# Two attention blocks on one core: exponential sums kept in the first block's own place, the last projection's products in turn, and the last norm's scalings queued behind other readers

## Chip, cores, metric

One core of a Trainium2 chip runs the whole program. The metric is the device time of one execution in microseconds (us). In what follows PE is TensorE (matmuls), DVE is VectorE, ACT is ScalarE, POOL is GpSimd, SP is the queue that issues most DMAs, PSUM is the memory that PE accumulates in (eight banks of 128 x 512 float32) and SBUF the on-chip memory that the other engines work in.

## The reference

The input is 8 images of 32 x 32 tokens with 512 channels, float32. Two layers run one after the other, each adding to its input:

```python
x = x + L0(gn(x))   # qkv = xt @ w_qkv; 16 heads of 32 channels; softmax(q k^T / sqrt(32)) v; @ w_proj + b
x = x + L1(gn(x))   # q, k, v by Wq, Wk, Wv; 4 heads of 128; scores + relative position logits; softmax; @ Wo
```

`gn` is a group norm over 32 groups of 16 channels. Softmax is over the 1024 keys.

## The kernel before

**Layout.** Activations are held transposed, channels on partitions: four chunks of 128 channels by 1024 tokens. Each 512 x 512 projection is done by a seven-product scheme (a two by two split of both operands with seven instead of eight half-size products). The sums of activations that it needs are made by `forming` (L343 to L371) as four DVE operations of 128 x 1024: s1, s2, a fresh a21 and s4. A product (`taken`, L385) reads one of these seven operands; product 5 needs s2, product 6 the fresh a21, product 2 needs s4, product 3 only a raw quarter. Results gather in three PSUM tiles x, y and z. Between two products of one tile another engine must have read it: `p1` (an ACT copy of x after product 0), `a` (a DVE add from y after product 5), `b` (the same after product 4), `p7` (an ACT copy of z after product 6). Class `Onto` (L536) adds the results to the running activations, and `put_out` (L1031) transposes 128 x 512 pieces on DVE and stores each with four DMAs, in the last image half of them from ACT's queue.

**Layer 0 attention** (`attention_0`, L632 to L702) walks, for each image, over 8 groups (4 chunks of heads by 2 halves of queries) and in each over 8 key blocks. For a block, `front` makes the scores of four heads by 8 matmuls into one PSUM tile `ps` of four banks, of which there is a single one, and ACT turns it into exponentials `e` (128 x 2048) at L653. A step later, `back` multiplies `e` with the values into `acc` (L664) and DVE adds `e` to the group's sum (L679). The tiles `e` have two buffers under the tag e0, and the sum `es` has one buffer of its own under es0. The first sum of a group, at its second block, reads the first two `e` and writes `es`. The later ones add one `e` to `es`. At the end `finish` sums `es` over partitions by a matmul (L689) and `normalise` (L602) makes the reciprocals and scales the result, its last operation being a POOL multiply (L630).

**Layer 1 attention** (`attention_1`, L754) does the same for four heads of 128, with smaller tiles; its last group also ends in `normalise`.

**Order.** PE always has other work to put beside an attention: `side_by_side` weaves the steps of layer 0 attention of image b with the projections of the images before and after. Within that, the framework's scheduler orders each engine's instructions when the program is made, by priority of tracing and by its own idea of when operands are ready. Two handles override it: `tc.issue_after(ins)` puts what is traced in it behind `ins` on that engine (order alone, no wait), and `tc.keep_in_program_order(ins)` puts one instruction behind everything traced before it on its engine. `by_columns` (L327) uses the latter while `in_place[0]` is set, for the four instructions of its next call.

**The end.** After the last attention nothing is left to weave. `after_last` (L1058) runs the last image's output projection by `in_two_parts` (L485): products 0 and 1 of both column halves u, which read query half 0, and then for each u `five_last` (L459) with products 5, 4, 6, 2, 3. The image before it goes through `after_1` (L1020) with the last image's second norm (`norm_1`, L978, `group_norm`, L265) woven in; the norm's four scalings (L304) are queued behind the newest layer 0 sum.

Of the kernel before, what the change touches and what calls it, by code (L numbers as in the profile page):

```python
# [27 lines left out]
def quick_path(  # L28
# [140 lines left out]


    ORDER = [0, 5, 1, 4, 6, 2, 3]
    FIRST_TWO, LAST_FIVE = [0, 1], [5, 4, 6, 2, 3]

    class Stream:

# [167 lines left out]
    def forming(x, name, room=None, behind=None, into=None):  # L343


        a11, a12 = x[:, :HC, :NB], x[:, HC:, :NB]
        a21, a22 = x[:, :HC, NB:], x[:, HC:, NB:]
        if room is not None:
            s1, s2, s4 = [room[:, i, :].rearrange("p (c n) -> p c n", n=NB) for i in range(3)]
        else:  # L350
            s1, s2, s4 = [
                mem.tile([P, HC, NB], F32, tag=f"form{i}", name=f"f{i}_{name}", bufs=1)
                for i in (1, 2, 4)
            ]
        fs = [a11, a12, s4, a22, s1, s2, a21]
        if into is not None:
            into.extend(fs)
        for i, (op, out, one, other) in enumerate((
            (nc.vector.tensor_add, s1, a21, a22),
            (nc.vector.tensor_sub, s2, s1, a11),  # L360
            (nc.vector.tensor_sub, a21, a11, a21),
            (nc.vector.tensor_sub, s4, a12, s2),
        )):

            late = None
            if behind is not None:
                late = behind[i]() if isinstance(behind, tuple) else behind()
            with tc.issue_after(late.ins) if late is not None else nullcontext():
                last_form[0] = op(out, one, other)
            yield 0  # L370
        return fs  # L371
# [110 lines left out]
        sink.c22(b, p7)  # L482
        yield HC

    def in_two_parts(x, m, sinks, name, room=None, done=lambda u: None, behind=None):  # L485

        early = [x[:, :HC, :NB], x[:, HC:, :NB]]
        p1s, fs = [], []
        sums = forming(x, name, room, behind, fs)

        def products():
            for u in range(2):
                stream.unit(m, False, u)
                p1s.append((yield from two_first(early, u, sinks[u], f"{name}_{u}")))

        def beside(u):
            if u == 0:
                yield from sums
                return

            with tc.issue_after(begun[0].ins):
                done(0)
            yield 0

        yield from woven(products(), (next(sums) for _ in range(2)), 0, 1)
        for u in range(2):
            stream.unit(m, False, u)
            yield from woven(five_last(fs, u, sinks[u], f"{name}_{u}", p1s[u]), beside(u), 0, 1)
        done(1)

    class Plain:
# [87 lines left out]
                hook if u else None,  # L599
            )  # L600

    def normalise(dst, acc_sums, name):  # L602

        su = mem.tile([P, NB], F32, tag="rec", name=f"su_{name}", bufs=2)
        nc.scalar.copy(su, acc_sums)  # L608
        turned = mem.tile([P, NB], F32, tag="rec", name=f"tu_{name}", bufs=2)
        nc.vector.transpose(turned, su)  # L610
        few = turned.rearrange("p (t c) -> p t c", c=32)[:, :, 0]
        rec = mem.tile([P, NB // 32], F32, tag="few", name=f"rc_{name}", bufs=2)
        nc.vector.reciprocal(rec, few)
        at = check_at[0]
        check_at[0] += 1
        nc.vector.tensor_tensor_reduce(
            out=few,
            in0=few,
            in1=rec,
            op0=ALU.add,  # L620
            op1=ALU.max,
            scale=1.0,
            scalar=0.0,
            accum_out=checks[:, at : at + 1],
        )
        nc.vector.transpose(  # L626
            su.rearrange("p (t c) -> p t c", c=32),
            rec.unsqueeze(2).to_broadcast([P, NB // 32, 32]),
        )
        nc.gpsimd.tensor_tensor(dst, dst, su, op=ALU.mult)  # L630

    def attention_0(q, k, v, b, blocks=range(NT)):  # L632

        steps = [(m, h, j) for m in (0, 2, 1, 3) for h in range(NH) for j in blocks]
        state = {}

        def front(m, h, j):
            name = f"0_{b}_{m}_{h}_{j}"
            ps = psum.tile([P, HB, NB], F32, tag="ps", name=f"ps_{name}", bufs=1)
            for i in range(2):  # L640

                some = slice(64 * i, 64 * i + 64)
                for r in range(HB):
                    rows = slice(r * D0, (r + 1) * D0)
                    nc.tensor.matmul(  # L645
                        ps[some, r, :],
                        k[m][rows, j * P + 64 * i : j * P + 64 * i + 64],
                        q[m][rows, h * NB : (h + 1) * NB],
                        start=True,
                        stop=True,  # L650
                    )
            e = mem.tile([P, HB, NB], F32, tag="e0", name=f"e_{name}", bufs=2)
            nc.scalar.activation(e, ps, AF.Exp, scale=D0 ** -0.5)  # L653
            return e

        def back(m, h, j, e):
            name = f"0_{b}_{m}_{h}_{j}"
            if j == blocks[0]:
                state["acc"] = psum.tile([P, NB], F32, tag="acc", name=f"acc_{name}", bufs=1)
                state["first"] = e  # L660
            acc = state["acc"]
            for r in range(HB):
                c0 = (m * HB + r) * D0
                nc.tensor.matmul(  # L664
                    acc[r * D0 : (r + 1) * D0, :],
                    v[:, j, c0 : c0 + D0],
                    e[:, r, :],
                    start=(j == blocks[0]),
                    stop=(j == blocks[-1]),
                )  # L670
            if j == blocks[1]:
                state["esum"] = mem.tile([P, HB, NB], F32, tag="es0", name=f"es_{name}", bufs=1)
                other = state["first"]
            elif j != blocks[0]:
                other = state["esum"]
            if j != blocks[0]:

                with tc.issue_after(reader[0].ins) if beside_norm[0] else nullcontext():
                    summed[0] = nc.vector.tensor_add(state["esum"], other, e)  # L679
            if j != blocks[-1]:  # L680
                return
            nc.scalar.copy(q[m][:, h * NB : (h + 1) * NB], acc)
            state["ended"] = (m, h, state["esum"])

        def finish(m, h, esum):
            name = f"0_{b}_{m}_{h}"
            su = psum.tile([P, NB], F32, tag="acc", name=f"sums_{name}", bufs=1)
            for r in range(HB):
                nc.tensor.matmul(  # L689
                    su[r * D0 : (r + 1) * D0, :],  # L690
                    ones[:, :D0],
                    esum[:, r, :],
                    start=True,
                    stop=True,
                )
            normalise(q[m][:, h * NB : (h + 1) * NB], su, name)

        pending = None
        for at in steps:
            if "ended" in state:  # L700
                finish(*state.pop("ended"))
            e = front(*at)  # L702
            if pending is not None:
                back(*pending)
            pending = (*at, e)
            yield 2
        back(*pending)
        yield 1
        finish(*state.pop("ended"))
# [44 lines left out]
    def attention_1(q, k, v, posT, b, beside=0):  # L754
# [38 lines left out]
        def finish(h, c, esum):  # L793
# [17 lines left out]
            su = psum.tile([P, HB, NB], F32, tag="ps", name=f"sums_{name}", bufs=1)[:, 0, :]  # L811
            nc.tensor.matmul(su, ones_r, greater, start=True, stop=False)
            nc.tensor.matmul(su, ones_r, rest, start=False, stop=True)
            normalise(q[:, h, c * NB : (c + 1) * NB], su, name)

        pending = None
        ending = []
# [240 lines left out]
    def after_last(b, st):  # L1058

        x = st["ao"]  # L1060
        xT = fetch(st["kept"], block(f"x2T_{b}"))
        sinks = [Onto(halves(xT, u), then=put_out(b, st, xT, u)) for u in range(2)]
        run(in_two_parts(x, WO, sinks, f"wo_{b}"))

    def woven(main, side, start, gap, places=(0,)):

        for at, cost in enumerate(main):
            if at >= start and (at - start) % gap in places:
                cost += next(side, 0)
            yield cost  # L1070
        yield from side
# [46 lines left out]
    def units(m, rows=False):  # L1118
        return [(m, rows, u, ORDER) for u in range(2)]

    def in_parts(m):
        return [(m, False, u, some) for some in (FIRST_TWO, LAST_FIVE) for u in range(2)]

    FIRST = units(WQ0) + units(WK0) + units(WV0, True)
    plan = [(m, m is WV0, u, ORDER) for u in range(2) for m in (WV0, WQ0, WK0)]
    for b in range(B + 1):
# [7 lines left out]
            plan += units(WQ1) + units(WK1) + units(WV1, True)  # L1134
        if b + 1 < B:
            plan += FIRST if b else units(WQ0) + units(WK0)[:1] + units(WV0, True)
    plan += in_parts(WO)

    states = [{} for _ in range(B)]
    load_first(states[0])  # L1140
# [21 lines left out]
    for b in range(B + 1):  # L1162
# [11 lines left out]
        if last is not None:  # L1174
            if past is not None:
                norm = norm_1(
                    b - 1, last, after=lambda: half_done[0], behind=lambda: summed[0]
                )
                if coming is not None:
                    norm = chain(norm, later(sums_1, b - 1, last))  # L1180
# [536 lines left out]
```

## Time and profile before

| what | value |
|---|---|
| median of 3 runs | 3826.51 us (3825.41 to 3826.73) |
| profiled execution, its own time | 3826.55 us |
| its span | 3824.8 us |
| mean granted PE clock | 0.998 |
| PE busy | 3786.5 us, 99% of the span |
| DVE busy | 2564.1 us, 67% |
| ACT busy | 1761.1 us, 46% |
| POOL busy | 658.5 us, 17% |

The span is from the first to the last instruction on the chip; the execution's own time is 1.75 us longer. A group row of the profile gives line, engine, operation, tiles written and read, shapes and count; then busy time and the mean of one; then the idle time of the engine just before these instructions and what ended it. A timeline row gives start and length in us, then the same names, with idle time in square brackets. A row of the table of waits reads "who waited <- for whom: total us, times, longest".

### The profile page before, as it was taken

Reading aid. Unit: us, or ns where it says so; the run is one execution under the profiler, and the core shown is the slowest. Engines: PE = TensorE matmul, PEld = TensorE weight load, DVE = VectorE, ACT = ScalarE, POOL = GpSimd, SP = SyncE. Lnnn points to the kernel's source line nnn. Section 1 sums busy time; section 2 is a strip of 40 time slices with the busy share of each in tenths; the row PEclk is TensorE's granted clock in tenths of the full one; section 3 lists DMA queues with packets and bytes.
Section 4 is the critical chain, followed back from the end, with each engine's and each line's share of the span. In section 5 each row is a group of like instructions: output and inputs, shape, how many; then the busy total and the mean of one; then the engine's idle time right before and its main releaser. Section 6 shows DMA issues by size and latency. Waiting matters only on the chain.

```text
span 3824.8 us, 79906 instructions
## 1 busy us (share of the span) xinstructions
PE 3786.5 (99%) x34478; PEld 1377.5 (36%) x34478; DVE 2564.1 (67%) x2966; ACT 1761.1 (46%) x1830; POOL 658.5 (17%) x398
## 2 busy tenths in 40 slices
PE   9999999999999999999999999999999999999998
PEld 4222244322443234432343323433234332334353
DVE  6778665686756866569665686656866568665544
ACT  2554544445444454444544445444454445553132
POOL 1342101131011310013111131111310112001201
PEclk9999999999999999999999999999999999999999
DMA  6132120242202312023120241103411033110311
GB/s 186 62 110 63 41 56 7 65 108 56 56 12 89 87 49 56 16 92 92 39 53 19 93 96 40 45 23 98 90 42 39 27 98 76 32 37 32 111 38 26
DMA packets 482985, 234.74 MB, mean 61 GB/s; under 512 B 269600, under 2 KB 461376, under 8 KB 481600
## 3 DMA queue, kind: packets, MB, share of 16 engines
q1 hardware_dynamic: 470992, 213.74, 20.5%
q0 software_dynamic: 2608, 13.70, 1.0%
q8 instruction: 274, 4.49, 0.5%
q10 hardware_dynamic: 9024, 2.10, 0.3%
q14 instruction: 87, 0.71, 0.1%
HBM read 170.72 MB, written 58.72 MB: 60 GB/s over the span
## 4 chain that ended last, share of the span: by engine, by line
PE 92%; DVE 4%; ACT 2%; issue 1%; DMA 0%; SPq 0%; POOL 0%; DVEq 0%; ACTq 0%; POOLq 0%
PE ps L645 13%; PE acc L664 12%; PE ps L764 12%; PE acc L776 12%; PE y_q L331 4%; PE y_v L331 4%; PE y_k L331 4%; PE ps L765 3%; PE x_q L331 3%; PE x_v L331 3%; PE z_k L331 3%; PE z_q L331 3%; PE x_k L331 3%; PE z_v L331 3%; ACT e L653 2%; DVE es L679 2%
## 5 line engine op out<-in xcount | busy, mean ns | idle before, releaser
L653 ACT ACTIVATE e<-ps 128x2048 f32<-128x2048 f32 x512 | 961.8, 1879 | 816.3 <-PE ps L645 631.3
L679 DVE TENSOR_TENSOR es<-es,e 128x2048 f32<-128x2048 f32 x384 | 891.1, 2321 | 380.7 <-ACT e L653 378.4
L645 PE MATMUL ps<-q,k 32*64 32x512 f32 x8192 | 577.7, 613 | 11.3 <-ACT e L653 11.3
L664 PE MATMUL acc<-e,v 128*32 128x512 f32 x4096 | 545.8, 604 | 0.0
L767 ACT ACTIVATE e<-ps 128x512 f32<-128x512 f32 x512 | 305.7, 597 | 507.2 <-PE ps L765 437.7
L764 PE MATMUL ps<-q,k 128*128 128x512 f32 x1024 | 525.0, 594 | 0.3 <-DVE posT L750 0.3
L776 PE MATMUL acc<-e,v 128*128 128x512 f32 x1024 | 522.0, 593 | 0.7 <-ACT e L767 0.7
L630 POOL TENSOR_TENSOR q<-q,su 128x512 f32<-128x512 f32 x128 | 201.6, 1575 | 1536.2 <-DVE su L626 1412.1
L787 DVE TENSOR_TENSOR es<-es,e 128x512 f32<-128x512 f32 x384 | 290.5, 757 | 251.3 <-ACT e L767 248.0
L765 PE MATMUL ps<-posT,sel 128*128 128x512 f32 x512 | 406.6, 794 | 0.0
L764 PEld LDWEIGHTS ps<-q,k 128*128 128x128 f32 x1024 | 192.5, 190 | 230.2 <-issue 218.5
L645 PEld LDWEIGHTS ps<-q,k 32*64 32x64 f32 x8192 | 120.4, 129 | 403.4 <-issue 211.8
L776 PEld LDWEIGHTS acc<-e,v 128*128 128x128 f32 x1024 | 193.1, 189 | 147.7 <-issue 92.6
L664 PEld LDWEIGHTS acc<-e,v 128*32 128x32 f32 x4096 | 81.3, 108 | 411.4 <-issue 364.1
L679 DVE TENSOR_TENSOR es<-e,e 128x2048 f32<-128x2048 f32 x64 | 177.3, 2770 | 31.9 <-ACT e L653 31.8
L610 DVE STREAM_TRANSPOSE tu<-su 128x512 f32<-128x512 f32 x128 | 90.6, 708 | 97.7 <-ACT su L608 96.1
L765 PEld LDWEIGHTS ps<-posT,sel 128*128 128x128 f32 x512 | 97.3, 190 | 122.5 <-issue 122.5
L608 ACT COPY su<-sums 128x512 f32<-128x512 f32 x128 | 74.9, 585 | 130.4 <-PE sums L689 80.6
L534 POOL TENSOR_TENSOR k<-b_k,p_k 128x512 f32<-128x512 f32 x32 | 51.2, 1601 | 479.4 <-ACT p_k L434 468.6
L750 DVE TENSOR_TENSOR posT<-pp,posT 32x512 fp32r<-32x512 f32 x128 | 111.9, 875 | 32.2 <-ACT posT L745 30.9
L745 ACT CAST posT<-pp 32x512 fp32r<-32x512 f32 x128 | 106.1, 829 | 46.4 <-PE pp L732 45.3
L534 POOL TENSOR_TENSOR v<-b_v,p_v 128x512 f32<-128x512 f32 x32 | 51.6, 1614 | 433.7 <-ACT p_v L434 433.7
(223 smaller groups left out, 4606.6 us busy)
## 6 DMA issues: line engine op xcount, KB each, us to landing
w_qkv<-ws_qkv SPq DMA_DIRECT2D x168, 128.0 KB, 2.3
d<-x0T SPq DMA_DIRECT2D x32, 512.0 KB, 3.2
x1T<-d SPq DMA_DIRECT2D x32, 512.0 KB, 5.9
d<-x1T SPq DMA_DIRECT2D x32, 512.0 KB, 3.6
x2T<-d SPq DMA_DIRECT2D x32, 512.0 KB, 6.4
w_qkv<-in_L_conv_w_qkv SPq DMA_DIRECT2D x126, 128.0 KB, 2.2
out<-ot SPq DMA_DIRECT2D x240, 64.0 KB, 2.0
xs<-in_x SPq DMA_DIRECT2D x224, 64.0 KB, 2.4
```

The source lines that it names most:

```text
L331: ins = nc.tensor.matmul(out[columns, :], weights[:, columns], moving, start=start, stop=stop, skip_group_check=open_sum,)
L630: nc.gpsimd.tensor_tensor(dst, dst, su, op=ALU.mult)
L645: nc.tensor.matmul(ps[some, r, :], k[m][rows, j * P + 64 * i : j * P + 64 * i + 64], q[m][rows, h * NB : (h + 1) * NB], start=True, stop=True,
L653: nc.scalar.activation(e, ps, AF.Exp, scale=D0 ** -0.5)
L664: nc.tensor.matmul(acc[r * D0 : (r + 1) * D0, :], v[:, j, c0 : c0 + D0], e[:, r, :], start=(j == blocks[0]), stop=(j == blocks[-1]),)
L679: summed[0] = nc.vector.tensor_add(state["esum"], other, e)
L750: nc.vector.tensor_sub(rest, logits, greater)
L764: nc.tensor.matmul(ps, k[h][:, keys], q[:, h, queries], start=True, stop=False)
L765: nc.tensor.matmul(ps, sel_flat[:, keys], posT[:, h, queries], start=False, stop=True)
L767: nc.scalar.activation(e, ps, AF.Exp, scale=1.0 / math.sqrt(D1))
L776: nc.tensor.matmul(acc, v[:, j, h * D1 : (h + 1) * D1], e, start=(j == 0), stop=(j == NT - 1),)
L787: added[0] = nc.vector.tensor_add(state["esum"], state["esum"], e)
```

## The change

Sums of layer 0: the two `e` buffers and the `es` buffer become one tile of three places. The first exponential of a group is written to one place and becomes the group's sum there; the later exponentials take turns in the other two; the next group's first one takes the next place in turn, and the old sum's place joins the turn behind it. The last output projection: products 0 of both halves, then products 1 of both, with three of `forming`'s operations traced beside them instead of two, then a new function `five_alone` with the order 5, 6, 4, 3, 2, each product's first four matmuls kept in program order; `forming`'s fourth operation is queued behind the add `a`. The very last `normalise` multiplies on DVE instead of POOL. In the last round the norm's scalings are queued behind the newest add `a` or `b` (`reader`) instead of the newest layer 0 sum.

```diff
-    FIRST_TWO, LAST_FIVE = [0, 1], [5, 4, 6, 2, 3]
+    FIRST_TWO, LAST_FIVE, LAST_ALONE = [0, 1], [5, 4, 6, 2, 3], [5, 6, 4, 3, 2]
...
-                late = behind[i]() if isinstance(behind, tuple) else behind()
+                late = behind[i] if isinstance(behind, tuple) else behind
+                late = late() if late is not None else None
...
+    def five_alone(fs, u, sink, name, p1):
+        product = taken(fs, u, False)
+        y = bank(f"y_{name}")
+        in_place[0] = True
+        product(y, 5, True)
+        a = snapshot("es1", f"a_{name}")
+        begun[0] = nc.vector.tensor_add(a, y, p1)
+        sink.early(p1, a)
+        yield HC
+        z = bank(f"z_{name}")
+        in_place[0] = True
+        product(z, 6, True)
+        p7 = snapshot("e1", f"p7_{name}")
+        nc.scalar.copy(p7, z)
+        yield HC
+        in_place[0] = True
+        product(y, 4, False)
+        b = snapshot("es1", f"b_{name}")
+        nc.vector.tensor_add(b, y, p1)
+        sink.middle(b)
+        yield HC
+        in_place[0] = True
+        product(z, 3, False)
+        sink.c21(z, a)
+        sink.c22(b, p7)
+        yield HC
+        in_place[0] = True
+        product(y, 2, False)
+        sink.c12(y, p1)
+        yield HC
...
         def products():
+            if in_turn:
+                base = stream.at + 1
+                parts = [two_first(early, u, sinks[u], f"{name}_{u}") for u in range(2)]
+                for i in range(4):
+                    stream.at = base + i % 2
+                    yield next(parts[i % 2])
...
-        yield from woven(products(), (next(sums) for _ in range(2)), 0, 1)
+        begin, rest = (3, five_alone) if in_turn else (2, five_last)
+        yield from woven(products(), (next(sums) for _ in range(begin)), 0, 1)
...
-        nc.gpsimd.tensor_tensor(dst, dst, su, op=ALU.mult)
+        engine.tensor_tensor(dst, dst, su, op=ALU.mult)
+
+    e_room = mem.tile([P, 3, HB, NB], F32, tag="e0", name="e_room", bufs=1)
+    turn, sum_at = [0, 1], [2]
...
-            e = mem.tile([P, HB, NB], F32, tag="e0", name=f"e_{name}", bufs=2)
+            at = turn.pop(0)
+            if j == blocks[0]:
+                turn.append(sum_at[0])
+                sum_at[0] = at
+            else:
+                turn.append(at)
+            e = e_room[:, at]
...
             if j == blocks[1]:
-                state["esum"] = mem.tile([P, HB, NB], F32, tag="es0", name=f"es_{name}", bufs=1)
-                other = state["first"]
-            elif j != blocks[0]:
-                other = state["esum"]
+                state["esum"] = state["first"]
...
-                    summed[0] = nc.vector.tensor_add(state["esum"], other, e)
+                    summed[0] = nc.vector.tensor_add(state["esum"], state["esum"], e)
...
+            end = (b, h, c) == (B - 1, H1 - 1, NH - 1)
+            normalise(
+                q[:, h, c * NB : (c + 1) * NB], su, name, nc.vector if end else nc.gpsimd
+            )
...
-        run(in_two_parts(x, WO, sinks, f"wo_{b}"))
+        run(in_two_parts(x, WO, sinks, f"wo_{b}", behind=(None, None, None, lambda: begun[0]), in_turn=True))
...
-    plan += in_parts(WO)
+    plan += in_parts(WO, LAST_ALONE)
...
-                    b - 1, last, after=lambda: half_done[0], behind=lambda: summed[0]
+                    b - 1,
+                    last,
+                    after=lambda: half_done[0],
+                    behind=lambda: (summed if here is not None else reader)[0],
```

More of the change, by code (lines that the diff above doesn't have):

```diff
@@ L483, in five_last, with in_two_parts @@
         yield HC
-    def in_two_parts(x, m, sinks, name, room=None, done=lambda u: None, behind=None):
+    def five_alone(fs, u, sink, name, p1):
[28 more added lines that the diff above has]
+        yield HC
+    def in_two_parts(
+        x, m, sinks, name, room=None, done=lambda u: None, behind=None, in_turn=False
+    ):
         early = [x[:, :HC, :NB], x[:, HC:, :NB]]
@@ L491, in products @@
         def products():
+            if in_turn:
[4 more added lines that the diff above has]
+                    yield next(parts[i % 2])
+                for part in parts:
+                    try:
+                        next(part)
+                    except StopIteration as end:
+                        p1s.append(end.value)
+                return
             for u in range(2):
@@ L503, in beside @@
             yield 0
-        yield from woven(products(), (next(sums) for _ in range(2)), 0, 1)
+        begin, rest = (3, five_alone) if in_turn else (2, five_last)
+        yield from woven(products(), (next(sums) for _ in range(begin)), 0, 1)
         for u in range(2):
             stream.unit(m, False, u)
-            yield from woven(five_last(fs, u, sinks[u], f"{name}_{u}", p1s[u]), beside(u), 0, 1)
+            yield from woven(rest(fs, u, sinks[u], f"{name}_{u}", p1s[u]), beside(u), 0, 1)
         done(1)
@@ L600, in project_rows, with normalise @@
             )
-    def normalise(dst, acc_sums, name):
+    def normalise(dst, acc_sums, name, engine=nc.gpsimd):
         su = mem.tile([P, NB], F32, tag="rec", name=f"su_{name}", bufs=2)
@@ L813, in finish @@
             nc.tensor.matmul(su, ones_r, rest, start=False, stop=True)
-            normalise(q[:, h, c * NB : (c + 1) * NB], su, name)
+            end = (b, h, c) == (B - 1, H1 - 1, NH - 1)
+            normalise(
+                q[:, h, c * NB : (c + 1) * NB], su, name, nc.vector if end else nc.gpsimd
+            )
         pending = None
@@ L1119, in units, with in_parts @@
         return [(m, rows, u, ORDER) for u in range(2)]
-    def in_parts(m):
-        return [(m, False, u, some) for some in (FIRST_TWO, LAST_FIVE) for u in range(2)]
+    def in_parts(m, last=LAST_FIVE):
+        return [(m, False, u, some) for some in (FIRST_TWO, last) for u in range(2)]
     FIRST = units(WQ0) + units(WK0) + units(WV0, True)
```

## The prediction

> **What bounds the kernel now.** I read the page's busy times first, then the table of waits, first for all engines and then for PE alone, then timelines of the places that it points at.
>
> ```profile
> PE 3786.5 (99%) x34478; PEld 1377.5 (36%) x34478; DVE 2564.1 (67%) x2966; ACT 1761.1 (46%) x1830; POOL 658.5 (17%) x398
> ```
>
> PE is the bound, so only PE's own standstills, and the start and the end where it has nothing to do, can be won: 3824.8 - 3786.5 = 38.3 us as busy time counts it. A VectorE microsecond saved elsewhere is worth nothing. Two answers of the table of waits say where a part of it lies, for all engines and for PE alone:
>
> ```profile
> ACT e L653 <- DVE es L679: 126.7, 40, 5.1
> ```
>
> ```profile
> PE ps L645 <- ACT e L653: 11.3, 15, 1.5
> ```
>
> ACT stood 126.7 us waiting for VectorE's sums before it could write an exponential; PE paid 11.3 us of that, in 15 pieces. One of them, in a timeline of layer 0 of the fourth image:
>
> ```profile
> 1289.86 1.11 PE L645 MATMUL ps<-q,k 32*64 32x512 f32 x16
> ...
> 1290.37 1.28 POOL L630 TENSOR_TENSOR q<-q,su 128x512 f32<-128x512 f32 x1 [11.55 <-DVE su L626]
> 1290.72 3.08 DVE L679 TENSOR_TENSOR es<-e,e 128x2048 f32<-128x2048 f32 x1
> ...
> 1293.92 1.88 ACT L653 ACTIVATE e<-ps 128x2048 f32<-128x2048 f32 x1 [5.05 <-DVE es L679]
> ...
> 1295.85 1.12 PE L645 MATMUL ps<-q,k 32*64 32x512 f32 x16 [0.45 <-ACT e L653]
> ```
>
> The scores at 1289.86 are those of a group's third block. Their exponential could start at about 1291.0, but its buffer is the first block's, which the group's first sum (es<-e,e) still reads until 1293.80. So it runs 2.9 us late, and since there is one `ps`, the fourth block's scores stand 0.45 us on PE. I numbered the 512 score sets: all 15 standstills lie before a fourth block, each time behind that first sum. By starts of PE instructions instead of modelled ends (a score set normally starts 0.54 us after the last set of projection matmuls) the 15 are 6.3 us in the first image, 0.7 in the second, 0.5 in each of the next five, 2.7 in the last: 12.1 us. The Trainium skill ("Trainium Kernel Development and Optimization", Performance Expectations) warns that matmul busy time is a bad metric because matmuls are pipelined; the trace bears it out here by 0.8 us of 12, and I take the starts.
>
> The other two places, PE's and VectorE's lines from the timelines of the last norm and of the last projection:
>
> ```profile
> 3566.72 1.92 PE L331 MATMUL y_wo<-f_ao,w_o 128*32 128x512 f32 x16 [0.69 <-DVE a_wo L420]
> ```
>
> ```profile
> 3788.20 3.64 PE L331 MATMUL x_wo<-q,w_o 128*32 128x512 f32 x30 [0.74 <-issue]
> ...
> 3789.47 1.27 POOL L630 TENSOR_TENSOR q<-q,su 128x512 f32<-128x512 f32 x1
> 3790.78 1.23 DVE L369 TENSOR_TENSOR f_wo<-q 128x1024 f32<-128x1024 f32 x1 [2.31 <-POOL q L630]
> ...
> 3792.53 1.92 PE L331 MATMUL x_wo<-q,w_o 128*32 128x512 f32 x16 [0.70 <-ACT p_wo L452]
> ...
> 3798.95 2.33 PE L331 MATMUL y_wo<-f_wo,w_o 128*32 128x512 f32 x17 [1.00 <-DVE a_wo L464]
> ```
>
> Each is a product that waits for another engine to have read its PSUM tile (p1 twice, a once), with nothing else for PE to do.
>
> **Part 1, sums in place.** Removed: the third exponential's wait for the first sum, since it now goes into the place of the last group's sum, which the matmul L689 has read two steps before. The exponentials of blocks four and later wait for the sum two blocks before, as now: the fourth's for the first sum, over at 1293.80, while its scores end near 1296.4. In all 15 cases the delayed exponential moves up (by 1.0 to 2.9 us) further than PE stood (0.5 to 1.6). ACT's and VectorE's counts stay the same. Added: the first sum writes over a tile that PE's products L664 read, so it waits for PE. These four follow directly behind the second block's scores and end 1.06 us after them, the exponential that the sum needs anyway ends 2.1 us after them: hidden by 1 us. If that cover were gone (products behind a filler product of 1.72 us) the sum would start 0.7 us late, with the rest of VectorE's queue behind it.
>
> Does the sum itself get shorter? Its row means:
>
> ```profile
> L679 DVE TENSOR_TENSOR es<-es,e 128x2048 f32<-128x2048 f32 x384 | 891.1, 2321 | 380.7 <-ACT e L653 378.4
> ...
> L679 DVE TENSOR_TENSOR es<-e,e 128x2048 f32<-128x2048 f32 x64 | 177.3, 2770 | 31.9 <-ACT e L653 31.8
> ```
>
> By the rows, in place is 0.45 us cheaper, 64 x 0.45 = 29 us of VectorE. The Trainium skill ("SBUF — State Buffer", Who interferes with whom) has another reason: a VectorE operation with two SBUF inputs and a GpSimd one that reads SBUF exclude each other. The trace sides with it: a first sum with POOL idle took 2.28 to 2.29 us, one that overlapped 0.9 us of POOL's scaling L630 took 3.04. That scaling stays beside it, so I count 0 instead of 29; either is off PE's path. Part 1: -12.1 us; bounds 0 (another wait ends last) and -12.1.
>
> **Part 2, the last norm's scalings.** At 3565.26 the fourth scaling (0.80 us) runs ahead of the add `a` at 3565.98, for which PE stands at 3566.72. Behind `reader` the last two scalings come after that add; it is ready when product 5 ends (3564.3), so product 4 follows product 1 at once: 0.87 us by starts. The earlier standstill there (0.46 us at 3562.39) has its scalings behind an old add and stays. The moved scalings delay the sums for the next projection: the first starts at 3569.32 behind `b`, the scalings would be done by 3567. Hidden. Nothing else is in the moved step (no DMA). -0.9; bounds 0 and -1.4.
>
> **Part 3, the last projection.** PE's products run from 3783.89 to 3814.93, 31.0 us. A product is 16 matmuls, 1.72 us; 14 are 24.1, the last sums' matmuls 0.7: 6.2 us of standing.
>
> - *New beginning.* Products 0, 0, 1, 1: each p1 copy (0.58) has a product beside it. PE reaches product 5 at 3783.89 + 0.67 + 4 x 1.72 + switches = 3791.5. It needs s2: the reciprocals are ready at 3788.11, DVE's multiply of 128x512 is 0.69 (row of the layer 1 sums), two sums at 1.22: 3791.3. Just in time; with POOL's 1.27 (at 3789.47, behind another POOL add) it would be 1.9 late. So the engine change carries this part.
> - *Then 5, 6, 4, 3, 2:* `a` has product 6 beside it, `b` product 3, p7 product 4. But product 6 needs the fresh a21, and VectorE has s1, s2, one output's add and transpose (1.4) and a21 (1.2 to 1.7) queued: ready at 3793.9 to 3794.3 against 3793.2, 0.7 to 1.1 late; `a` is queued behind the second output: 0.3 more. I take 1.2. VectorE's work from 3788.1 on sums to 19.9 us (end 3808.0), so it has little room. The pinned matmuls let nothing pass: if the DVE queue is worse, up to 3 us. Ten products: 3791.5 + 17.2 + 1.2 = 3809.9, which is 5.0 earlier.
> - *Tail.* Before, three outputs (12 DMAs of 64 KB) go out after 3814.7, at the speed of this row, about 1.9 us an output; packets end at 3821.9 and 2.9 us of closing follow.
>
> ```profile
> 3819.00:3820.00 1.00, 0.00 (x0) 0.00 (x0) 0.00 (x0) 0.00 (x0) 0.00 (x0) 0.50 1.08 147
> ```
>
> After, product 3's two outputs are ready before product 2's one, but the three still crowd: first store 0.1 us before PE ends (add and transpose 1.4 after a start at -1.5), 0.75 until packets flow, 5.7 of draining: 6.3 behind PE's end instead of 6.9. -0.6.
>
> Part 3: -5.6; bounds -2 and -8.
>
> **Sum.** -12.1 - 0.9 - 5.6 = -18.6. From the profiled execution's own 3826.55 (span 3824.8 and 1.75 outside) that is 3807.95; the median, 3826.51, is the same within 0.04. I say 3808.0.
>
> **Rivals.**
>
> - *The wait moves on* (16%). VectorE is busy 83.07 of the 90 us from 790 to 880, where a later image's standstill lies. With the exponential gone ahead, the scheduler may queue other VectorE work differently, so that a later sum or an `a`/`b` is late. Half of part 1 comes back: 3814. For: that queue; against: the first sum ends 2.6 us before its next reader needs it.
> - *The last projection gains little* (14%). VectorE's output adds and transposes ahead of s2 or a21 eat the part: -1 instead of -5.6, 3812.5. For: 19.9 us of work in 20; against: outputs are not ready before 3790.0, s1 and s2 are traced earlier.
> - *Slower* (5%). In-place writes bind VectorE to PE: if the products L664 stand behind two filler products (3.44 us), each first sum waits 2.4 us for PE, with VectorE's queue behind it. From 0.4 us of PE standing in each of 64 groups it passes the 18.6 won and 7.7 more: at 0.7 us 3853. Against: in the timelines those products follow their scores directly.
> - *Not what it says* (2%). If the one tile of three places were ordered as a whole, each exponential would wait for the sum before: 1.88 + 2.3 + 0.2 = 4.4 us a step against 3.3 to 3.8 in the first image, some 50 us more. Against: at 3793.65 VectorE transposes one part of x2T while POOL writes another (3792.56 to 3794.88).
>
> **How the numbers follow.** The likeliest (63%) gives 3808, by its bounds 3803 to 3812. The range takes in the second rival and the better half of the first: 3803 to 3815. A difference under 0.2% (7.7 us, here 3818.9) could not be told from none. Faster 0.92; same 0.04 (both losses of the first two rivals together); slower 0.04, rounded from the last two.
>
> **What would show it.** The 15 waits of PE for ACT's exponential gone, ACT's 126.7 us for the sums down to under 60; first sums still near 2.8 us; product 4 of the last norm's projection without its 0.69; a last projection of 26 us from first to last matmul, with the waits for p1 and `a` gone and one for a21 before product 6; a tail behind PE of some 9 us. Wrong would be: new waits of PE at L645 for later exponentials, a first sum released by L664, PE standing at pinned products for more than 3 us.

## The result and the profile after

| | before | after |
|---|---|---|
| median | 3826.57 us (9 runs, 3825.41 to 3828.88) | 3815.11 us (9 runs, 3814.71 to 3817.06) |
| profiled execution, its own time | 3826.55 us | 3816.57 us |
| its span | 3824.8 us | 3815.0 us |

The ratio is 0.9971, with a 95% interval of 0.9962 to 0.9979: 11.5 us less, 0.3%. The forecast was 18.6 less (3808.0), with a range up to 3815. So the direction was right, and somewhat more than a third of the gain is missing. The profiled execution of the kernel after took 3816.57, 1.5 above its median; the last section shows where most of that lies. One execution of e11_behind below ran at a granted clock of 0.862 and took 7350.46 us; it is left out of that run's median, and all other times are of executions at 0.997 to 0.999.

First the busy times of the kernel after:

```profile
PE 3786.7 (99%) x34478; PEld 1376.4 (36%) x34478; DVE 2574.9 (67%) x2967; ACT 1761.8 (46%) x1830; POOL 660.0 (17%) x397
```

PE's work is the same within 0.2 us, and the span is 9.8 shorter: everything won is time in which PE stood still. In the table of waits for PE, the kernel after has these rows that bear on the three parts:

```profile
PE y_wo L331 <- DVE f_wo L370: 0.8, 1, 0.8
PE z_wo L331 <- ACT p_wo L500: 0.8, 2, 0.4
...
PE y_q L331 <- DVE a_q L421: 0.6, 1, 0.6
...
PE sums L746 <- DVE e_room L736: 0.4, 1, 0.4
...
PE ps L698 <- ACT e_room L713: 0.2, 1, 0.2
```

The last row answers to the 11.3 us that PE stood at layer 0's scores; 0.2 is left. In ACT's own table the 126.7 us for the sums have become 15.7:

```profile
ACT e_room L713 <- DVE e_room L736: 15.7, 5, 4.0
```

The timeline of the same third and fourth blocks as before the change (fourth image) shows how:

```profile
1284.57 1.11 PE L698 MATMUL ps<-q,k 32*64 32x512 f32 x16
...
1285.44 3.06 DVE L736 TENSOR_TENSOR e_room<-e_room 128x2048 f32<-128x2048 f32 x1
...
1285.79 1.88 ACT L713 ACTIVATE e_room<-ps 128x2048 f32<-128x2048 f32 x1 [2.22 <-PE ps L698]
...
1290.04 1.11 PE L698 MATMUL ps<-q,k 32*64 32x512 f32 x16
```

The exponential now starts 1.2 us behind its scores, while the first sum still runs, instead of 4.1. From one score set to the next it is 5.47 us, before 5.99: the half microsecond is won. The first sum is no shorter (3.06 beside POOL's scaling), as the forecast said; over all 448 sums of layer 0 the mean is 2407 ns, before (891.1 + 177.3) / 448 = 2385:

```profile
L736 DVE TENSOR_TENSOR e_room<-e_room 128x2048 f32<-128x2048 f32 x448 | 1078.6, 2407 | 396.4 <-ACT e_room L713 393.7
```

**Where the lead comes and goes.** I took the start of each of the 512 score sets in both traces; the difference is PE's lead over the kernel before. At the first set it is -1.7. It grows at all 15 fourth blocks, but in later images it is partly lost again: in five images 0.5 is won at the fourth block and 0.3 lost nine score sets later, and in the last image 1.6 is lost. It is 7.6 after the last layer 0 attention, 8.6 after the last norm, where product 4 (y_wo) now follows product 1 (x_wo) without idle time:

```profile
3556.48 1.90 PE L331 MATMUL x_wo<-q,w_o 128*32 128x512 f32 x16
3558.20 1.90 PE L331 MATMUL y_wo<-f_ao,w_o 128*32 128x512 f32 x16
```

This is what takes 0.3 of it back in one of the five images (the fourth); first the kernel before, then the kernel after, at the same instructions:

```profile
1334.15 2.24 DVE L679 TENSOR_TENSOR es<-es,e 128x2048 f32<-128x2048 f32 x1
...
1335.56 1.90 PE L331 MATMUL x_q<-x1T,w_q 128*32 128x512 f32 x16
1336.32 0.67 DVE L420 TENSOR_TENSOR a_q<-y_q,p_q 128x512 f32<-128x512 f32 x1
...
1337.27 1.90 PE L331 MATMUL y_q<-f_xn,w_q 128*32 128x512 f32 x16
```

```profile
1328.80 2.25 DVE L736 TENSOR_TENSOR e_room<-e_room 128x2048 f32<-128x2048 f32 x1
...
1329.75 1.90 PE L331 MATMUL x_q<-x1T,w_q 128*32 128x512 f32 x16
1330.96 0.68 DVE L421 TENSOR_TENSOR a_q<-y_q,p_q 128x512 f32<-128x512 f32 x1
1331.57 2.27 DVE L736 TENSOR_TENSOR e_room<-e_room 128x2048 f32<-128x2048 f32 x1
1331.70 1.92 PE L331 MATMUL y_q<-f_xn,w_q 128*32 128x512 f32 x16
```

VectorE runs without a gap in both, in the same order: a sum, then the add `a`, then a sum. Before, the sum began 1.41 us ahead of PE's filler product x_q, after only 0.95: PE has come half a microsecond closer to an engine that is itself without a gap here, so `a` ends when product x_q has been issued (1331.64), not earlier, and y_q starts 1.95 behind x_q instead of 1.71.

**The last projection.** From first to last product 28.45 us, before 31.0, forecast 26.0. Its timeline, POOL, VectorE, ACT and PE together:

```profile
3779.67 4.01 POOL L593 TENSOR_TENSOR x2T<-x2T,p_wo 128x512 f32<-128x512 f32 x2 [8.81 <-issue]
...
3780.35 2.19 DVE L370 TENSOR_TENSOR f_wo<-q 128x1024 f32<-128x1024 f32 x1
...
3782.58 2.18 DVE L370 TENSOR_TENSOR f_wo<-f_wo,q 128x1024 f32<-128x1024 f32 x1
...
3784.82 1.92 PE L331 MATMUL y_wo<-f_wo,w_o 128*32 128x512 f32 x16 [0.77 <-DVE f_wo L370]
...
3787.15 2.81 ACTq L1103 DMA_DIRECT2D out<-ot  x4
...
3790.00 0.58 ACT L500 COPY p_wo<-z_wo 128x512 f32<-128x512 f32 x1 [8.74 <-DMA out<-ot]
3790.64 0.64 PE L331 MATMUL z_wo<-q,w_o 128*32 128x512 f32 x4 [0.37 <-ACT p_wo L500]
```

Two things are there that the forecast did not have: s1 and s2 take 2.19 and 2.18 us instead of 1.22, beside two POOL adds, and the copy p7 stands behind four output DMAs in ACT's own queue. Its operand z_wo had been ready since about 3788.5.

### The profile page after: what moved, and what is told of

Same layout as the page of the kernel before. It is cut to its first block, busy times and chain, and to the rows that moved or that the text cites. A ratio compares the mean times of both kernels' runs of the same rounds, so it can differ in the third digit from the quotient of the medians.

```text
span 3815.0 us, 79937 instructions
## 1 busy us (share of the span) xinstructions
PE 3786.7 (99%) x34478; PEld 1376.4 (36%) x34478; DVE 2574.9 (67%) x2967; ACT 1761.8 (46%) x1830; POOL 660.0 (17%) x397
## 5 line engine op out<-in xcount | busy, mean ns | idle before, releaser
L736 DVE TENSOR_TENSOR e_room<-e_room 128x2048 f32<-128x2048 f32 x448 | 1078.6, 2407 | 396.4 <-ACT e_room L713 393.7
L713 ACT ACTIVATE e_room<-ps 128x2048 f32<-128x2048 f32 x512 | 961.8, 1879 | 788.5 <-PE ps L698 744.2
L724 PE MATMUL acc<-e_room,v 128*32 128x512 f32 x4096 | 545.8, 604 | 0.0
L724 PEld LDWEIGHTS acc<-e_room,v 128*32 128x32 f32 x4096 | 81.3, 108 | 411.4 <-issue 364.1
L583 POOL TENSOR_TENSOR q<-b_q,p_q 128x512 f32<-128x512 f32 x32 | 67.9, 2121 | 255.2 <-ACT p_q L435 255.2
```

Source lines behind the costliest of these rows:

```text
L583: nc.gpsimd.tensor_tensor(self.dst[1][1], s(b), s(p7), op=ALU.add)
L724: nc.tensor.matmul(acc[r * D0 : (r + 1) * D0, :], v[:, j, c0 : c0 + D0], e[:, r, :], start=(j == blocks[0]), stop=(j == blocks[-1]),)
L736: summed[0] = nc.vector.tensor_add(state["esum"], state["esum"], e)
```

## The experiments

Theory A: the change does its three things, and the shortfall is a full VectorE in layer 0 (3.7 us), POOL's adds beside s1 and s2, and p7 behind ACT's DMAs. Rival B: part 1 is paid in full and the other parts give some of it back.

**Each part alone.** `e1_sums` is the kernel before with the three places, `e2_projection` with the new last projection and the normalise on VectorE, `e3_norm` with the norm's scalings behind the readers.

> Part 1 alone (the kernel before with the sums kept in the first block's place). Theory A, 'the wait moves on in part': the 15 standstills (12.1 us by starts) go, and 3.7 us of new ones come in the layer 0 attentions of later images, where VectorE's queue is full: about 8.4 us less, near 3818.2, with a_q or e_room adds as what PE waits for in images 3 to 7. Rival B, 'part 1 is paid in full and the last projection takes some of it back': 12 us less, near 3814.5, and the new waits absent because they belong to another part.

> The last projection's change alone, with its normalise on VectorE (sums and norm as in the kernel before). Theory A: first to last product 28.5 us instead of 31.0, less up to 1.4 us of a longer tail: 1.2 to 2.6 us less, 3824.0 to 3825.4; PE waits for s2 by about 1 us and twice for p7. Rival B: nothing or a loss, 3826.5 to 3827.5.

> The norm's scalings behind the readers, alone. Both theories: the one wait of 0.69 us for an add a before product 4 goes, 0.9 us less, 3825.6, too little for the medians to show with certainty; the trace shows it by starts of PE's products.

| run | median | against before (3826.15) | ratio, 95% interval |
|---|---|---|---|
| e1_sums | 3817.45 us (11 runs) | -8.7 | 0.9977 [0.9968, 0.9986] |
| e2_projection | 3823.70 us (13 runs) | -2.45 | 0.9994 [0.9986, 1.0003] |
| e3_norm | 3825.44 us (13 runs) | -0.7 | 0.9998 [0.9990, 1.0006] |

The kernel before was run again beside each set of experiments; its medians lie between 3826.07 and 3826.57 us. So half a microsecond between medians of different sets, here and below, says little.

The parts sum to -11.9, the whole change gave -11.5: within what the medians can tell the parts do not disturb each other, and B falls. The last two medians alone would not prove a gain; their traces do. In e2_projection first to last product is 28.5 us, in e3_norm PE's lead is 0.6 through all of layer 0 and 1.6 after the last norm. In e1_sums the lead grows by 12.7 us in 16 steps (12.4 at the 15 fourth blocks, and one place where 0.36 is regained) and falls by 3.9 in nine, the same places as in the full change. So the returned 3.9 belongs to part 1 itself. The table of waits of e1_sums names VectorE for 1.2 us of it; the small losses are hidden in this table by the modelled ends of PE's matmuls:

```profile
PE y_q L331 <- DVE a_q L420: 0.6, 1, 0.6
PE sums L696 <- DVE e_room L686: 0.6, 2, 0.4
```

**Is it VectorE's load?** Half of six sums in seven left out (so the denominators of two heads in four are too small), in the kernel after and as a control in the kernel before:

```diff
-                    summed[0] = nc.vector.tensor_add(state["esum"], state["esum"], e)
+                    k = HB if j == blocks[1] else HB // 2
+                    summed[0] = nc.vector.tensor_add(state["esum"][:, :k], state["esum"][:, :k], e[:, :k])
```

> The changed kernel, but of layer 0's sums only each group's first is made whole; the six later ones add two of the four heads (half of the columns), so the softmax denominators of the other two heads are left too small. VectorE loses 384 x 1.2 = 461 us. Theory A (the new waits of images 0 to 7 come from VectorE's full queue): the 3.7 us of new waits in layer 0's attentions go, and no wait for a or for e_room is left there: 3.7 us less, 3811.4, or somewhat better still. Rival B (they come from the order of the queue, not its load, or from PE's own pace): the waits stay where they are, within 1 us of 3815.1.

> The kernel before with the same relief of VectorE as in the run on the changed one: of layer 0's sums only each group's first is whole, the later six add two of the four heads, so two heads' denominators are too small. If the 15 standstills of the kernel before are a chain (the third exponential waits for the first sum, whatever the load), they stay: 10 to 12 us of them, and the time falls by at most 3 us, 3823.5 to 3826. If they too come from VectorE's load, they go: near 3812 to 3814.

e8_half_after: 3807.71 us (5 runs), 7.4 less than the kernel after. VectorE is busy 2172.9 us (57%). PE's lead now only grows up to the last group: 11.5 at the fourth block of the seventh image, 14.3 at that of the eighth's third group. None of the nine losses above is left, and no row for a_q or e_room stands in PE's waits. So VectorE's sums are the cause of these losses. Whether it is their amount or their place in the queue this run can't tell, since it also shortens the very sums that stand ahead of the adds. It gave more than the 3.7 expected. 1.1 us comes in the first image, where PE waits 0.4 us for VectorE's add `b` in the kernels before and after, and a product and a group's summing matmuls cut into each other behind it; here neither is so. And the scheduler changed an order: in the kernel after, layer 1's summing matmuls cut into two score sets of layer 0's last group, and here they don't. First the kernel after, then the run:

```profile
3378.31 1.07 PE L698 MATMUL ps<-q,k 32*64 32x512 f32 x2
3379.31 1.12 PE L854 MATMUL sums<-es,ones 128*128 128x512 f32 x2
```

```profile
3371.46 1.02 PE L855 MATMUL sums<-es,ones 128*128 128x512 f32 x2
```

Two matmuls of a score set alone take 1.0 us before the next instruction, where all 16 together take about 1.05; the two places of this kind are 1.2 us each, 2.4 together. With the 3.7 and the 1.1 that is 7.2 of the 7.4.

e9_half_before: 3819.01 us (17 runs), ratio 0.9982 [0.9974, 0.9989], 7.4 less than before: my expectation of at most 3 was wrong. The same two cuts give 2.4 of it, and the same place in the first image 1.1. Of the 15 standstills ten stay, 7.9 of 11.3 us:

```profile
PE ps L645 <- ACT e L653: 7.9, 10, 1.5
```

The five of 0.5 us in images 3 to 7 go, because the first sum, still whole, now runs clear of POOL's scaling: 2.37 us (at 1288.42, fourth image) where it took 3.08: VectorE, relieved, handed over the scale factors earlier, and POOL's scaling was over at 1287.40. The exponential still waits for all of it (4.30 us of idle, ended by that sum), as a chain must; it only ends early enough. So the standstill was chain and sum length together, and VectorE's load, through the moment of POOL's scaling, decided the length.

**Sums behind the adds.** If only the order in VectorE's queue were at fault, putting every sum behind the newest add would mend it:

```diff
-                with tc.issue_after(reader[0].ins) if beside_norm[0] else nullcontext():
+                with tc.issue_after(reader[0].ins) if reader[0] is not None else nullcontext():
```

> The changed kernel with every layer 0 sum queued behind the newest add a or b of a projection, not only beside the norm. If the new waits are the adds a standing behind a sum in VectorE's queue, those for a_q (0.33 us an image in five images, and 0.6 in the last) go: about 2 us less, 3813. If the queue is merely full, the sums come late instead and the exponentials or the sums' matmuls wait: no gain or up to 5 us more, with PE waits at the scores or at the sums of layer 0.

3835.36 us (median of 12 runs, ratio 1.0023 [1.0015, 1.0031]): 20 us worse than the kernel after. But order does count. No row for a_q is left among PE's waits, and the five losses of 0.3 us in images 3 to 7 are gone, though VectorE has as much to do as in the kernel after (2574.3 us busy, there 2574.9). What makes the run slow is new: PE waits for the sums instead, before the matmul that closes a group:

```profile
PE sums L746 <- DVE e_room L736: 17.9, 12, 2.2
```

Six of these places cost 1.83 to 1.86 us each by starts, 11.1 together. One of them, VectorE's lines and then PE's:

```profile
974.66 0.69 DVE L429 TENSOR_TENSOR b_v<-y_v,p_v 128x512 f32<-128x512 f32 x1 [4.70 <-PE y_v L331]
...
978.10 2.29 DVE L736 TENSOR_TENSOR e_room<-e_room 128x2048 f32<-128x2048 f32 x1
```

```profile
980.53 1.06 PE L746 MATMUL sums<-e_room,ones 128*32 128x512 f32 x8 [2.18 <-DVE e_room L736]
```

The exponential that this sum adds had ended at 968.37. VectorE was not full: it stood idle for 4.70 us, because the sum was queued behind an add whose product PE had not made yet. Five other places cost 0.9 each, 4.4 together. There VectorE has no gap for 9 us ahead of the matmul, and the sum now stands behind three of `forming`'s operations: a queue without room does pay for the new order. So both count, the amount of VectorE's work and its order, and the 20 us do not show that the order can't be bettered; a pin at the places of the five losses alone was not tried. Nor was a fourth place, so that out-of-place sums could keep a buffer of their own beside three exponentials.

**What kept the last projection from 26 us.** Three edits of the kernel after. In `e4_gathers` POOL's add of p1 goes behind its add of `a`:

```diff
-        sink.early(p1, a)
+        g = sink.gather(0, 1, a)
+        with tc.issue_after(g.ins):
+            sink.gather(1, 0, p1)
```

In `e5_queue` ACT issues output DMAs only for the last three outputs, SP all others; `e6_both` has both edits.

```diff
-                queue = nc.scalar if b == B - 1 and a % 2 else nc.sync
+                queue = nc.scalar if b == B - 1 and u and (n or h) and a % 2 else nc.sync
```

> The changed kernel with the two POOL adds of p1 (4.0 us together, beside s1 and s2) moved behind the add of a, when the first two sums are over. Theory A (s1 and s2 are 2.19 and 2.18 us because POOL's adds read SBUF beside them; the run with the multiply on POOL had s2 alone at 1.22): s1 and s2 at 1.22 each, PE's wait of 0.77 before product 5 gone, about 1.0 us less, 3814.1. The waits for p7 stay. Rival B (the two sums are slow for another reason, such as the operand's place): 2.2 us each again, and no gain. Rival C: the gain is lost again before product 6 or at p7 (0.4 grows to 1.4), since ACT's queue is late by itself: same time, 3815.1.

> The changed kernel with ACT's queue issuing output DMAs only for the last half's last three outputs; SP issues all the others. Theory A (the p7 copies are late because ACT is still issuing DMAs): both waits for p7 (0.37 and 0.40 in the waits, 0.6 and 0.9 by starts) go, 1.2 to 1.5 us less at PE's last product, near 3813.7, if SP keeps up. Rival B: the copies are late for PE's product 6 itself, and the waits stay. Rival C: SP's queue, now with 20 DMAs before the last three outputs, becomes late, and the tail behind PE grows from 11.2 to 12.5 us or more: 3815 to 3817.

> Both edits. Theory A: all three waits of PE inside the projection go, first to last product 26.0 to 26.3 us instead of 28.45; 2.2 us less than the changed kernel if the tail stays, near 3812.9. Rival: the tail behind PE takes it back, since the outputs crowd: 3815.

| run | median | first to last product | PE's end to the end of the span |
|---|---|---|---|
| after | 3815.11 us | 28.45 us | 11.2 us |
| e4_gathers | 3813.17 us (5 runs) | 27.1 us | 11.0 us |
| e5_queue | 3816.58 us (10 runs) | 26.9 us | 14.9 us |
| e6_both | 3815.60 us (10 runs) | 25.9 us | 14.5 us |

VectorE's timeline of e4_gathers, with POOL idle until 3785:

```profile
3778.77 1.22 DVE L370 TENSOR_TENSOR f_wo<-q 128x1024 f32<-128x1024 f32 x1
3780.03 1.22 DVE L370 TENSOR_TENSOR f_wo<-f_wo,q 128x1024 f32<-128x1024 f32 x1
```

Both sums are back at 1.22 and the wait for s2 is gone. One matmul of product 5 starts 7.7 us behind the first product and the others from 8.2 on (forecast 7.6, after 9.5). All five times of e4_gathers lie below the fastest of the kernel after. In e6_both, where p7 is free too, the ten products end at 25.9: the forecast of 26 holds once its two assumptions do, in part by luck, since two of its other terms were wrong in opposite directions (next section). But SP, now with 26 of the last image's 32 output DMAs instead of 16, can't issue them in time, and ACT's last six take longer too (6.85 us instead of 5.44), here in the timeline of e5_queue:

```profile
3802.19 6.85 ACTq L1103 DMA_DIRECT2D out<-ot  x6
```

The tail grew by 3.6 and 3.3 us, more than the 1.5 and 2.6 that the projection won. So e5_queue's rival C was right: some of ACT's share in the issuing is needed, and its price is p7.

**A middle way.** `e10_three`: the adds moved as in e4_gathers, and ACT spared only the two outputs that stand directly ahead of a p7 copy.

```diff
-                queue = nc.scalar if b == B - 1 and a % 2 else nc.sync
+                queue = nc.scalar if b == B - 1 and (n, h, u) not in [(0, 0, 1), (1, 0, 0)] and a % 2 else nc.sync
```

> The changed kernel with POOL's adds of p1 behind the add of a, and ACT issuing no output DMA for the two outputs whose DMAs stand directly ahead of a p7 copy in its queue (SP issues all four of each; 18 DMAs instead of 12 before the last three outputs are shared as before). Theory A (p7 late behind ACT's DMAs, tail set by how the last DMAs are shared out): both remaining waits for p7 (0.24 and 0.28; about 1.2 us by first to last product, 27.1 to 26.0) go and the tail stays near 11: 1.0 to 1.2 us less than with the adds moved alone (3813.2), 3812.0. Rival: SP's 4 more DMAs come late, the tail grows by 1 us or more, 3813 or worse.

3812.55 us (5 runs, 3812.47 to 3813.24), ratio to before 0.9964 [0.9951, 0.9977]: 2.6 us less than the kernel after and the fastest here that leaves nothing out. First to last product 26.3 us, tail 11.1, no wait for p7 among PE's. It is 0.6 better than e4_gathers by the medians (0.9 when each is set against its own runs of the kernel before), not the 1.0 to 1.2 expected. SP issues 14 DMAs ahead of the last three outputs here, not the 18 that the expectation counted.

**The engine of the last normalise.** `e7_pool` is the kernel after with that multiply back on POOL.

> The changed kernel with the very last normalise's multiply back on POOL. If VectorE's multiply carries the new beginning: s2 later by the 0.6 us of the longer multiply and by what POOL's queue adds (two adds of 2.0 us each may stand ahead of it), so PE's wait before product 5 grows from 1.0 to between 1.6 and 5 us and the time to between 3815.7 and 3819. If the wait for s2 is set by the two slow sums alone and POOL's adds then move out of their way (s1 and s2 at 1.22 instead of 2.19): the multiply costs 0.6, the sums win 1.9, and the time is 1 us less, near 3814.

3815.70 us (8 runs, 3814.80 to 3816.20), 0.6 more than the kernel after, which the medians alone don't prove: by the traces the two theories were each half right. POOL, VectorE and PE in its timelines:

```profile
3779.44 1.28 POOL L679 TENSOR_TENSOR q<-q,su 128x512 f32<-128x512 f32 x1
3780.68 1.28 POOL L593 TENSOR_TENSOR x2T<-x2T,p_wo 128x512 f32<-128x512 f32 x1
```

```profile
3780.76 2.28 DVE L370 TENSOR_TENSOR f_wo<-q 128x1024 f32<-128x1024 f32 x1 [2.33 <-POOL q L679]
3783.08 1.22 DVE L370 TENSOR_TENSOR f_wo<-f_wo,q 128x1024 f32<-128x1024 f32 x1
```

```profile
3784.36 1.92 PE L331 MATMUL y_wo<-f_wo,w_o 128*32 128x512 f32 x16 [1.79 <-DVE f_wo L370]
```

The sums start later, but one of POOL's two adds is over by then, and s2 runs alone. PE's wait grows from 0.77 to 1.79, product 4 now waits 0.5 for `a`, and first to last product is 29.9 us, 1.5 more than in the kernel after; the medians show 0.6 of it. The s1 row is the cleanest measure of the exclusion: 2.28 = 1.22 + 1.06, and POOL's add runs beside it for 1.2 us.

## Why the prediction was right in direction and too large

The gain is 7.1 us short of the forecast: 3.4 in part 1, 3.2 in part 3, 0.2 in part 2, and 0.4 by which the parts alone sum to more than the whole.

- **Part 1, forecast -12.1, measured -8.7 (e1_sums).** The mechanism and the price of the 15 standstills were right: the lead grows by 12.4 us at them. What failed is the step "In all 15 cases the delayed exponential moves up (by 1.0 to 2.9 us) further than PE stood", which I took as the whole gain. It answers only whether this wait goes; the rival "the wait moves on" named the full VectorE (83.07 of 90 us busy) and gave it 16%, for half of part 1. It should have been in the sum: where VectorE's queue runs without a gap and a sum stands ahead of `a`, PE gets no more than there is in reserve, and the reserve could be read, as the gap between the end of `a` and PE's need for it (1336.99 against 1337.27 in the kernel before: 0.28 us, while 0.52 was to be won). 3.9 us came back. By this reading each of images 3 to 7 wins some 0.2 instead of 0.5, which is what was measured (0.51 - 0.33, 0.52 - 0.26, and so on). That is 1.6 of the 3.9 in e1_sums. The other four losses, most of them in the last image, I did not read in this way; of them the runs show only that they go when the sums are shortened.
- **No cheaper sums: right.** In place they take 2407 ns in the mean against 2385, each group's first one 2.79 us against 2.77. The rule of the Trainium skill that I had set against the row means ("SBUF — State Buffer", Who interferes with whom) decided rightly; 29 us less of VectorE would have been wrong.
- **Part 2, forecast -0.9: right.** The lead grows by 0.9 in the kernel after and in e3_norm; the median of e3_norm moved by 0.7.
- **Part 3, forecast -5.6, measured -2.45 (e2_projection).** The term "two sums at 1.22: 3791.3, just in time" was mis-sized by 1.93 us: I had used the exclusion rule for the first sums of layer 0 and not here, though the same trace shows POOL's adds of p1 next to them. That made product 5 about 1.0 late. The pinned summing matmuls, which cut into product 0 behind its first two matmuls, cost 1.44 us of PE (3775.33 to 3776.98, less 0.21 for the two), not 0.67. "p7 has product 4 beside it" overlooked that an ACT copy queues behind ACT's DMA issues; that was 0.6 and 0.9 us by starts. The allowance of 1.2 us for a late a21 was not needed: a21 was in time. So where p7 and the sums are free (e6_both) the pinned matmuls' 0.8 too little and a21's 1.2 too much nearly cancel, which is the luck in its 25.9.
- **The tail, forecast -0.6.** Nothing of it is shown. PE's end to the end of the span was 9.8 us before and 11.2 after, but it is 11.0 and 10.6 in e1_sums and e3_norm, which leave the projection as it was, and 10.0 in e2_projection, which has the new one. It varies between executions by more than the term.
- **The start.** The profiled execution of the kernel after was 1.7 us behind at the first score set. The change does not make this: in the profiled executions of all eleven experiments, seven of them with the whole change, the first score set came from 0.1 us later to 0.6 earlier than before. The last section shows what differs.

Of the signs that I named, these came true: the waits at L645 and for p1 and `a` gone, ACT's 126.7 far under 60, first sums near 2.8 us. The named wrong sign "new waits of PE at L645" did not come; the waits moved to `a_q` and to the sums' matmul, where I had not looked. No first sum waited for PE's products, and "slower" had nothing to stand on.

## What to carry to other kernels

When a wait of the bounding engine is taken away, ask what each other engine has in reserve at that place: read how long before its need the next operand is ready, and count no more than that unless the queue in front of it also moves. A sum of durations for a new stretch must be made with the neighbours that will really run beside it (here POOL's adds beside VectorE's sums), and a compute copy on an engine that also issues DMAs must be costed behind them. Pinning an order in a queue can cure one wait and make dearer ones: ask of the pin whether what stands ahead is ready by then (in e11_behind it was not, for 4.70 us). Taking work out of the queue, as e8_half_after shows, removed these waits in layer 0 without new ones there.

## What the hardware showed that I had not expected

- **The granted clock's start.** PE's clock rises to full in the first 30 us at different moments. Columns of these rows: window, its length, PE, PEld, DVE, ACT and POOL busy (instructions), granted PE clock, DMA share, GB/s. Before, then after:

```profile
24.00:26.00 2.00, 2.00 (x32) 1.03 (x29) 2.00 (x3) 0.00 (x0) 0.00 (x0) 0.76 0.85 129
26.00:28.00 2.00, 2.00 (x44) 1.31 (x40) 2.00 (x4) 0.00 (x0) 0.00 (x0) 1.00 0.41 61
```

```profile
24.00:26.00 2.00, 2.00 (x24) 0.86 (x17) 2.00 (x3) 0.00 (x0) 0.00 (x0) 0.50 0.78 116
26.00:28.00 2.00, 2.00 (x24) 0.83 (x17) 2.00 (x4) 0.00 (x0) 0.00 (x0) 0.50 0.62 94
```

  PE counts as busy in all four, but at 0.50 it starts 24 matmuls in 2 us instead of 44 at 1.00. In e1_sums the clock is 0.74 already from 22 to 24 us. The nine times of the kernel after spread over 2.4 us; that the clock's start makes most of it is likely but not shown, since only the profiled execution shows its clock in this detail.
- **DMA issue as queue time.** An output DMA of 64 KB took ACT's queue 0.37 to 1.61 us to issue while others were under way (four of them 2.81 us, six 5.44, in the kernel after), and a compute instruction behind them waited that long.
